# Folding products placed inside a mixture's routing head, weight rows from counting ends, and gathers queued in order of use, in a four-layer graph network

## The chip, the cores and the metric

The kernel runs on one core of one Trainium2 chip. The metric is the device time of a whole execution in microseconds (us). Five engines work side by side, each through its own queue in order: TensorE (PE, matrix products; its weight loads are listed as PEld), VectorE (DVE), ScalarE (ACT), GpSimd (POOL) and SyncE (SP). DMA transfers are issued from the queues of SP, ACT and POOL. A profile shows, for PE, the clock that was granted as a share of full speed.

## The reference, cut to what matters

512 nodes with 768 features pass four layers. Each layer adds a graph part, a mixing (attention) part and a feed-forward part to `x`. The feed-forward parts of layers 0 and 2 are mixtures of 8 experts, with 384 hidden features, in which each node goes to its one best expert:

```python
xn = _layernorm(x)
# layers 0 and 2: one expert per node (layer 0 has a router bias and gelu, layer 2 silu)
logits = xn @ Ws + bs
probs  = softmax(logits);  e = argmax(probs);  p = max(probs)
x = x + p * (act(xn @ W1[e] + b1[e]) @ W2[e] + b2[e])
# layer 1, graph part: relational attention, twice (heads = 4, then 1)
xr = einsum('nd,rdf->rnf', x, W);  qi = xr[etype, dst] @ q;  kj = xr[etype, src] @ k
# layer 3, graph part
ft = einsum('nhd,ed->nhe', h, W_fc);  a1 = (ft * attn_l).sum(-1);  a2 = (ft * attn_r).sum(-1)
```

Layer 3 ends with a mixture of 16 experts in which each expert takes 64 nodes, plus a shared expert. All arithmetic is float32 unless an intermediate is exact in a narrower type.

The scores `xr @ q` and `xr @ k` of layer 1 equal `x @ (W q)` and `x @ (W k)`. The products `W q`, `W k` depend on weights alone. The kernel computes them once per convolution and calls this folding. Layer 3's `W_fc` with `attn_l`, `attn_r` is folded in the same way.

## The kernel before

One program runs the four layers one after the other; `x` stays in on-chip memory. PE's instruction stream is in order, and a scheduler fixes the order on every engine when the program is built, from the program's order and its dependencies. `tc.issue_after(ins)` ties what is traced inside it behind `ins` on the same engine.

**Weights.** `wp` (in `Net.__init__`) is a ring of six slots of 1152 KB, tag `w`. `self.w` loads the next slot through SP's queue (L257); a load waits until the products that read that slot's former content are done. The mixtures take slots from the same ring for gathered weights. `self.gate` and `self.before` make the fifth SP load after a mixture's gathers wait for the last of these.

**PSUM.** `self.ps()` hands out eight banks in turn.

**A mixture, `moe(f, act, xn, bs)`** is called as f0 (layer 0) and f2 (layer 2). Its head:

- it normalizes `x` into `xn` (L401-405), writes `xn` to DRAM as `f_there` (L755), loads the router weights `wg` (L750), transposes `xn` into `xnT` (`to_fm`, transposes at L354), and forms the logits `lo` (L341, L333, L767);
- DVE marks each node's best expert in `g`, `gb` (L769-779). Two small products with `lower` and `onesb` (L333) count the nodes before each node, and all nodes, per expert. Out of the counts come `bl`, the blocks of 128 nodes that an expert needs, `end`, the running sum of them, and `beg`; and `place`, the position of each node in the list sorted by expert (L787-802);
- `spot` (L820) marks that position in a 0/1 matrix of 128 x 1408 for each of the four tiles of nodes. 44 products with `number` turn it round into `who`, the node numbers of each block (L825, L827);
- `own` and `low` (L832-839) find out which expert owns each of the 11 possible blocks, and so `rows`, the weight rows to fetch;
- `gT`, `wayT`, `diag` (L853-871) carry the probabilities, and later put results back in their places.

Nine blocks are always run, two more under a branch (L942). `fetch(i)` issues three gathers on POOL: the nodes `xb` (L887), then the expert's first and second weights (L881, by `rows`), and transposes `xb` to `xbT`. `first` is the first product, `middle` the activation with its transposes, `second` the second product, whose result goes to DRAM as `f_back` (L924). Round `i` of the loop runs `middle(i)`, `first(i+1)`, `fetch(i+2)`, a bias product, `second(i)`. After the loop four gathers `yb` bring the results back in node order (L949). 16 products with `wayT` and 8 with `diag` (L957, L960) finish them, and DVE and ACT add them to `x` and normalize for the next layer, tile by tile (L967-996).

**After f0** `fold` (L1195 and on) gives `products`: six loads of `g1_t1` through SP, and 36 products of 32 columns by 384 at L1204, accumulated into two banks and copied by ACT to `vt` (L1208). Then `to_fm` transposes the new `xn` into `xnT`; `turn` transposes `vt` into `V1` (L1216); and `mix1` starts with the products of `xnT` and `m1_wqkv`. `gnn1` folds its second convolution with the same function.

**After f2** `last_two` calls `fold3` first: two small loads, `wf` and `lr`, through POOL's queue (L1587, L1589), one product of them, and twelve copies of 64 x 2 by DVE into `V` (L1598). Then it transposes `xn` into `xnT`, and `gnn3` multiplies it with `V` (L341).

Of the kernel before, what the change touches and what calls it, by code (L numbers as in the profile page):

```python
# [10 lines left out]
F32 = mybir.dt.float32  # L11
BF16 = mybir.dt.bfloat16
I16 = mybir.dt.int16
I32 = mybir.dt.int32
AF = mybir.ActivationFunctionType
OP = mybir.AluOpType
# [153 lines left out]
class Net:  # L170
# [173 lines left out]
    def narrow_tm(self, four, n):  # L344

        p = self.ps()
        for t in range(NT):
            self.acc(p[:, t * n : (t + 1) * n], [(four[:, t * P : (t + 1) * P], self.fours[:, :n])])
        return p[:, : NT * n].rearrange("p (t n) -> p t n", t=NT)
# [390 lines left out]
    def moe(self, f, act, xn, bs=None):  # L740
# [5 lines left out]
        with ExitStack() as c:  # L746
# [4 lines left out]
            xnT = one.tile([P, KC, N], F32, name="xnT")  # L751
# [15 lines left out]
            nc.vector.tensor_copy(lo, self.narrow_tm(loT, E))  # L767
# [14 lines left out]
            self.acc(p[:, :32], [(self.lower, gf)])  # L782
            self.acc(p[:, 32:64], [(self.onesb, gf)])
# [10 lines left out]
            nc.vector.tensor_tensor_scan(end, self.ones[:, :E], bl, 0.0, OP.mult, OP.add)  # L794
            beg = one.tile([P, E], F32, name="beg")
# [26 lines left out]
            for i in range(NB):  # L822
                self.acc(p[:, 2 * i : 2 * i + 2], [(spot[:, t, i * P : (i + 1) * P], self.number[:, t, :]) for t in range(NT)])
# [3 lines left out]
            nc.vector.tensor_copy(who, sums)  # L827

            own = one.tile([P, NB, E], F32, name="own")
            low = one.tile([P, NB, E], F32, name="low")  # L830
            iob = self.io16[:, :NB, None].to_broadcast([P, NB, E])
            nc.vector.tensor_tensor(own, iob, end[:, None, :].to_broadcast([P, NB, E]), OP.is_lt)  # L832
            nc.vector.tensor_tensor(low, iob, beg[:, None, :].to_broadcast([P, NB, E]), OP.is_ge)
            nc.vector.tensor_mul(own, own, low)
            nc.vector.tensor_mul(low, own, self.io8[:, None, :].to_broadcast([P, NB, E]))
            which = one.tile([P, NB, 1], F32, name="which")
            nc.vector.tensor_reduce(which, low, AX.X, OP.add)
            rows = one.tile([P, NB], I32, name="rows")
            nc.vector.tensor_scalar(rows, which[:, :, 0], float(P), self.me, OP.mult, OP.add)
# [39 lines left out]
            def pick(table, i):  # L879
                t = self.wp.tile([P, WB], F32, tag="w", name="w") if i < NA else two.tile([P, WB], F32, name="wm")  # L880
                nc.gpsimd.indirect_dma_start(out=t, out_offset=None, in_=table.rearrange("e p n -> (e p) n"),  # L881
                                             in_offset=bass.IndirectOffsetOnAxis(ap=rows[:, i : i + 1], axis=0))
                return t

            def fetch(i):
                xb = two.tile([P, D], F32, name="xb", bufs=3)
                nc.gpsimd.indirect_dma_start(out=xb, out_offset=None, in_=there,  # L887
                                             in_offset=bass.IndirectOffsetOnAxis(ap=who[:, i : i + 1], axis=0))
                w1 = pick(d[f + "_w1"], i).rearrange("p (k n) -> p k n", k=KC)
                w2 = pick(d[f + "_w2"], i).rearrange("p (k n) -> p k n", k=3)  # L890
                xbT = two.tile([P, KC, P], F32, name="xbT")
                for k in range(0, KC, 3):
                    p = self.ps()
                    for j in range(3):
                        self.tr(p[:, j * P : (j + 1) * P], xb[:, (k + j) * P : (k + j + 1) * P])
                    self.copy(xbT[:, k : k + 3, :], p[:, :HW].rearrange("p (k n) -> p k n", k=3))
                return xbT, w1, w2

            def first(i, xbT, w1):
                p = self.ps()  # L900
                self.acc(p[:, :HW], [(xbT[:, k, :], w1[:, k, :]) for k in range(KC)])
                h = two.tile([P, HW], F32, name="h" if i < NA else "hm")
                self.copy(h, p[:, :HW])
                return h
# [10 lines left out]
            def second(i, hT, w2):  # L915
                y = two.tile([P, D], F32, name="y")
                for nb in range(2):
                    p = self.ps()
                    at = slice(nb * HW, (nb + 1) * HW)
                    self.acc(p[:, :HW], [(hT[:, k, :], w2[:, k, at]) for k in range(3)])  # L920
                    self.copy(y[:, at], p[:, :HW])
                if i != NA - 1:
                    o = i * P if i < NA else (i - 1) * P
                    nc.scalar.dma_start(back[o : o + P, :], y)  # L924
                return y
# [3 lines left out]
            xbT, w1, w2 = fetch(0)  # L929
            h = first(0, xbT, w1)  # L930
            ahead = fetch(1)
            for i in range(NA - 1):
                hT = middle(i, h)
                xbT, w1, after = ahead
                h = first(i + 1, xbT, w1)
                if i + 2 < NA:
                    ahead = fetch(i + 2)
# [4 lines left out]
            with tc.If(count > NA):  # L942
                for i in range(NA, NB):
                    xbT, wa, wb = fetch(i)
                    second(i, middle(i, first(i, xbT, wa)), wb)
# [245 lines left out]
    def fold(self, wq, l, H):  # L1191
# [4 lines left out]
        def products(temp):  # L1196
            vt = temp.tile([96, D], F32, name="vt")
            ps = [self.ps() for _ in range(2)]
            for kb in range(2):
                ws = [self.wr(d[f"g1_t{l}"][r, kb]) for r in range(3)]  # L1200
                for j in range(3):
                    for nb in range(2):
                        for r in range(3):
                            nc.tensor.matmul(ps[nb][32 * r : 32 * r + 32, :HW], wq[:, 3 * kb + j, :],  # L1204
                                             ws[r][:, j, nb * HW : (nb + 1) * HW],
                                             start=kb + j == 0, stop=kb == 1 and j == 2)
            for nb in range(2):
                nc.scalar.copy(vt[:, nb * HW : (nb + 1) * HW], ps[nb][:96, :HW])  # L1208
            return vt
# [9 lines left out]
        return products, turn  # L1219
# [93 lines left out]
    def gnn1(self, V1, xnT):  # L1313
        nc, tc, d = self.nc, self.tc, self.d
        with ExitStack() as c:
# [31 lines left out]
            products, turn2 = self.fold(self.padded(one.tile([P, KC, 32], F32, name="wq"), 2, 1), 2, 1)  # L1347
# [4 lines left out]
            with tc.tile_pool(name="g1_vt", bufs=1) as temp:  # L1352
                vt = products(temp)
# [161 lines left out]
    def last_two(self, xn, xnT, out):  # L1515
# [5 lines left out]
        with ExitStack() as c:  # L1521
            one = c.enter_context(tc.tile_pool(name="m3_one", bufs=1))
            two = c.enter_context(tc.tile_pool(name="m3_two", bufs=2))
            V = self.fold3(one)
# [57 lines left out]
    def fold3(self, one):  # L1582
# [9 lines left out]
        p = self.ps()  # L1592
        self.acc(p[:, : 2 * H], [(wf, lr)])
        for a in range(2):
            at = slice(64 * a, 64 * a + 64)
            for f in range(KC):
                h = 2 * f + a
                nc.vector.tensor_copy(V[at, f, h : h + H + 1 : H], p[at, h : h + H + 1 : H])  # L1598
        return V
# [332 lines left out]
def tile_net(ctx, tc, dram, at, out, only=ALL):  # L1932
# [30 lines left out]
    with tc.tile_pool(name="L1", bufs=1) as pool, ExitStack() as keep:  # L1963
        right = keep.enter_context(tc.tile_pool(name="L1n", bufs=1, side="right"))
        xn = right.tile([P, NT, D], F32, name="xn")
        net.moe("f0", AF.Gelu, xn, "f0_bs")
        right = keep.enter_context(tc.tile_pool(name="L1a", bufs=1, side="right"))
        xnT = pool.tile([P, KC, N], F32, name="xnT")
# [3 lines left out]
        products, turn = net.fold(net.wq1, 1, 4)  # L1972
        vt = products(right)
# [15 lines left out]
    with tc.tile_pool(name="f3_x", bufs=1) as last:  # L1989
# [4 lines left out]
        with tc.tile_pool(name="f3_n", bufs=1) as p2:  # L1994
            xn = p2.tile([P, NT, D], F32, name="xn")
            net.moe("f2", AF.Silu, xn)
            there = net.last_two(xn, xnT, xn)
# [26 lines left out]
```

## Time and profile before

| | us |
|---|---|
| median of 3 runs | 4235.73 |
| lowest, highest | 4232.37, 4238.52 |
| the profiled execution's own time | 4235.37 |
| its span, first to last instruction | 4233.6 |
| PE busy | 4092.9 |
| DVE busy | 1295.3 |
| ACT busy | 664.4 |
| POOL busy | 274.2 |

The span is a little shorter than the time of the same execution. A row of the timeline gives start, duration, engine, line, operation, `out<-in` with the shapes, the number of instructions that are merged in it and, in brackets, the idle time before it with what ended that. The float32 products show as two rows each: a product of 128 x 128 with 384 columns, counted x12, is six products. A row of waits gives who waited for whom: total, times, longest. A row of windows gives the busy time of PE, PEld, DVE, ACT and POOL in a stretch with their instruction counts, then the granted PE clock, the busy share of the DMA engines and GB/s.

### The profile page before, as it was taken

The numbers are of one execution on the slowest core, as the hardware profiler recorded it, in microseconds if no ns is written. First come the engines' busy times: TensorE is split into PE (matmuls) and PEld (weight loads), VectorE is DVE, ScalarE is ACT, GpSimd is POOL, SyncE is SP. The second block draws the span as 40 slices with busy tenths as digits, with TensorE's granted clock in tenths as the row PEclk, the third lists the DMA queues.
The fourth block names the chain that finished last, engine by engine and source line by source line (L and its number), as shares of the span: only waits on it lengthen the run. The fifth ranks groups of instructions, "written<-read, shape, count | busy, mean of one in ns | idle before, by whom it ended". The sixth has DMA issues, their size and how long they took to land. (4 is left out here: it accounts for less than half of the span.)

```text
span 4233.6 us, 40102 instructions
## 1 busy us (share of the span) xinstructions
PE 4092.9 (97%) x16356; PEld 2094.4 (49%) x16356; DVE 1295.3 (31%) x3096; ACT 664.4 (16%) x1258; POOL 274.2 (6%) x325
## 2 busy tenths in 40 slices
PE   9989999999989999999999999989989999999999
PEld 3434555554455566755644444445654444444444
DVE  8871111112432135613220101034751222122211
ACT  1221200001312223511200000012620000000000
POOL 1120000001022010000000000021110000000000
PEclk9999999999999999999999999989999999999999
DMA  3111011111047112211211111064069999999998
GB/s 111 53 64 56 23 45 67 68 56 54 18 178 291 42 56 72 109 45 56 98 44 57 55 56 53 4 237 155 12 282 427 427 427 426 427 427 427 420 425 366
DMA packets 99549, 710.90 MB, mean 168 GB/s; under 512 B 12608, under 2 KB 12945, under 8 KB 29985
## 3 DMA queue, kind: packets, MB, share of 16 engines
q1 hardware_dynamic: 78064, 601.20, 35.2%
q0 software_dynamic: 16816, 95.80, 6.0%
q10 hardware_dynamic: 4480, 11.28, 0.7%
q8 instruction: 132, 2.16, 0.2%
q14 instruction: 57, 0.46, 0.0%
HBM read 685.68 MB, written 22.54 MB: 167 GB/s over the span
## 5 line engine op out<-in xcount | busy, mean ns | idle before, releaser
L1851 PE MATMUL ps<-w,xg 128*64 128x384 f32 x3072 | 567.1, 489 | 0.3 <-DVE xg L249 0.3
L1851 PEld LDWEIGHTS ps<-w,xg 128*64 128x64 f32 x3072 | 235.8, 137 | 287.0 <-issue 257.5
L1473 PE MATMUL ps<-aT,w 128*128 128x512 f32 x864 | 372.3, 592 | 0.0
L1867 PE MATMUL ps<-w,hT 128*64 128x384 f32 x1536 | 319.4, 490 | 3.4 <-ACT hT L251 1.9
L333 PE MATMUL ps<-xnT,w 128*128 128x512 f32 (+1 forms) x732 | 321.5, 596 | 0.2 <-ACT xnT L251 0.2
L1473 PEld LDWEIGHTS ps<-aT,w 128*128 128x128 f32 x864 | 164.4, 190 | 203.4 <-issue 202.1
L333 PE MATMUL ps<-w,xnT 128*128 128x384 f32 x672 | 221.6, 487 | 0.2 <-DVE xnT L249 0.2
L333 PEld LDWEIGHTS ps<-xnT,w 128*128 128x128 f32 (+1 forms) x732 | 134.3, 184 | 174.7 <-issue 171.1
L1867 PEld LDWEIGHTS ps<-w,hT 128*64 128x64 f32 x1536 | 131.8, 137 | 166.7 <-issue 137.1
L410 DVE TENSOR_TENSOR x<-x,ps 128x384 f32<-128x384 f32 x224 | 123.5, 553 | 262.7 <-PE ps L333 192.7
L333 PE MATMUL ps<-C,parts 128*128 128x512 bf16 x864 | 188.6, 380 | 2.7 <-DVE inv L1495 2.7
L333 PE MATMUL ps<-w,hT 128*128 128x384 f32 x552 | 184.7, 490 | 3.9 <-ACTq L942 3.9
L514 PE MATMUL ps<-ohd,so 128*128 128x512 bf16 x816 | 184.1, 386 | 2.7 <-DVE so L511 2.7
L333 PEld LDWEIGHTS ps<-w,xnT 128*128 128x128 f32 x672 | 127.2, 190 | 88.4 <-issue 4.7
L1483 DVE TENSOR_TENSOR aT<-inv,ps 128x512 f32<-128x512 f32 x72 | 49.5, 687 | 365.6 <-PE ps L333 365.6
L1854 ACT ACTIVATE h<-ps 128x384 f32<-128x384 f32 x64 | 31.4, 490 | 781.5 <-PE ps L1851 781.5
L1855 DVE TENSOR_TENSOR h<-h,ps 128x384 f32<-128x384 f32 x64 | 35.4, 554 | 371.6 <-PE ps L1851 371.6
L333 PEld LDWEIGHTS ps<-w,hT 128*128 128x128 f32 x552 | 103.3, 190 | 81.2 <-ACT xbT L251 7.6
L333 PE MATMUL ps<-w,aT 128*128 128x384 f32 (+1 forms) x416 | 139.6, 486 | 0.5 <-DVE aT L249 0.4
L333 PE MATMUL ps<-xnT,sw 128*128 128x512 f32 x288 | 139.3, 615 | 0.0
L333 PEld LDWEIGHTS <-parts 128*128 128x128 bf16 x864 | 84.7, 98 | 108.1 <-issue 8.8
L514 PEld LDWEIGHTS <-so 128*128 128x128 bf16 x816 | 79.7, 99 | 107.6 <-DVE so L511 14.3
(511 smaller groups left out, 4826.7 us busy)
## 6 DMA issues: line engine op xcount, KB each, us to landing
w<-in_f_Wg_dram SPq DMA_DIRECT2D x128, 1152.0 KB, 14.6
w<-in_f_Wu_dram SPq DMA_DIRECT2D x128, 1152.0 KB, 14.7
w<-in_f_Wd_dram SPq DMA_DIRECT2D x128, 1152.0 KB, 14.6
w<-in_g_w_dram SPq DMA_DIRECT2D x54, 1152.0 KB, 5.1
w<-in_m_wqkv_dram SPq DMA_DIRECT2D x24, 1152.0 KB, 8.3
w<-in_g_t_dram SPq DMA_DIRECT2D x12, 1152.0 KB, 6.3
w<-in_m_wp_dram SPq DMA_DIRECT2D x8, 1152.0 KB, 5.2
ea<-in_edge_attr_dram SPq DMA_DIRECT2D x34, 256.0 KB, 2.7
```

The source lines that it names most:

```text
L333: i = self.nc.tensor.matmul(out, a, b, start=n == 0, stop=n == len(pairs) - 1)
L410: self.nc.vector.tensor_add(xs, xs, p)
L514: nc.tensor.matmul(p, so[:, n, t * P : (t + 1) * P], ohd[:, j, :], start=False, stop=j == (g + 1) * HJ - 1)
L1473: nc.tensor.matmul(outs[nb * 3 + f], w[:, k, f * P : (f + 1) * P], xT[:, k, :], start=first and k == 0, stop=last and k == KC - 1)
L1483: nc.vector.tensor_mul(aT[:, f, :], inv[:, r, :], p)
L1851: nc.tensor.matmul(p[a * 64 : a * 64 + 64, :HW], xg[:, k, a * CAP : (a + 1) * CAP], ws[b][a][:, k, :], start=k == 0, stop=k == KC - 1)
L1854: nc.scalar.activation(h, pg[:, :HW], AF.Silu)
L1855: nc.vector.tensor_mul(h, h, pu[:, :HW])
L1867: nc.tensor.matmul(po[nb][a * 64 : a * 64 + 64, :HW], hT[:, f * P + a * 64 : f * P + a * 64 + 64], wd[a][:, f, nb * HW : (nb + 1) * HW], s ...
```

## The change

Four things change, in both mixtures unless said otherwise.

1. `fold` returns `in_parts` in place of `products`: the same 36 products in three parts of 6, 12 and 18. In f0 they are handed to `moe` as `fill`, and run after the logits' products, after the two counting products, and after the `spot` products, each tied to its place with `issue_after`. Their six loads move ahead of the mixture's on SP. In `gnn1` the three parts run one after the other where `products` ran. `xnT` is made outside `moe` and passed in.
2. `fold3` splits in two. Its loads and the memset of `V` come ahead of f2's mixture on POOL's queue; the product and the twelve copies run in round 2 of f2's loop (`later`).
3. `rows` comes from `end` alone: `which` counts how many of the first seven ends a block's number has reached. `own` is made from `which` after `who`. One comparison, two multiplications and the intermediate `low` fall away. The 44 `spot` products run tile by tile instead of block by block, in one accumulation.
4. The gathers of the always-run blocks are queued with `send`, each behind the former: first weights of block 0, nodes 0, nodes 1, first weights 1, second weights 0, and then in each round nodes `i+2`, first weights `i+2`, second weights `i+1`. Transposing (`turned`) is separate from fetching.

```diff
-    def moe(self, f, act, xn, bs=None):
+    def moe(self, f, act, xn, xnT, bs=None, fill=None, later=None):
...
+            logits = self.narrow_tm(loT, E)
+            nc.vector.tensor_copy(lo, logits)
+            last = self.told
+            if fill:
+                with tc.issue_after(last):
+                    last = fill(0)
...
+            with tc.issue_after(last):
+                self.acc(p[:, :32], [(self.lower, gf)])
+                last = self.acc(p[:, 32:64], [(self.onesb, gf)]).ins
+            if fill:
+                with tc.issue_after(last):
+                    last = fill(1)
...
+            nc.vector.tensor_tensor(over, self.io16[:, :NB, None].to_broadcast([P, NB, E - 1]),
+                                    end[:, None, : E - 1].to_broadcast([P, NB, E - 1]), OP.is_ge)
+            nc.vector.tensor_reduce(which, over, AX.X, OP.add)
+            nc.vector.tensor_scalar(rows, which[:, :, 0], float(P), self.me, OP.mult, OP.add)
...
-            for i in range(NB):
-                self.acc(p[:, 2 * i : 2 * i + 2], [(spot[:, t, i * P : (i + 1) * P], self.number[:, t, :]) for t in range(NT)])
+            with tc.issue_after(last):
+                for t in range(NT):
+                    for i in range(NB):
+                        last = nc.tensor.matmul(p[:, 2 * i : 2 * i + 2], spot[:, t, i * P : (i + 1) * P],
+                                                self.number[:, t, :], start=t + i == 0,
+                                                stop=t == NT - 1 and i == NB - 1).ins
+            if fill:
+                with tc.issue_after(last):
+                    last = fill(2)
...
-            nc.vector.tensor_tensor(own, iob, end[:, None, :].to_broadcast([P, NB, E]), OP.is_lt)
-            nc.vector.tensor_tensor(low, iob, beg[:, None, :].to_broadcast([P, NB, E]), OP.is_ge)
-            nc.vector.tensor_mul(own, own, low)
-            nc.vector.tensor_mul(low, own, self.io8[:, None, :].to_broadcast([P, NB, E]))
...
+            with tc.issue_after(placed):
+                nc.vector.tensor_tensor(own, self.io8[:, None, :].to_broadcast([P, NB, E]),
+                                        which.to_broadcast([P, NB, E]), OP.is_equal)
...
+            def send(fn, *args):
+                nonlocal sent
+                with tc.issue_after(sent) if sent else nullcontext():
+                    t, i = fn(*args)
+                sent = i.ins
+                return t
...
-            xbT, w1, w2 = fetch(0)
-            h = first(0, xbT, w1)
-            ahead = fetch(1)
+            w1 = send(pick, W1, 0)
+            xb = send(gather, 0)
+            ahead = send(gather, 1)
+            h = first(0, turned(xb), w1)
+            w1 = send(pick, W1, 1)
+            w2 = send(pick, W2, 0)
+            xbT = turned(ahead)
             for i in range(NA - 1):
                 hT = middle(i, h)
-                xbT, w1, after = ahead
                 h = first(i + 1, xbT, w1)
                 if i + 2 < NA:
-                    ahead = fetch(i + 2)
+                    xb = send(gather, i + 2)
+                    w1 = send(pick, W1, i + 2)
+                after = send(pick, W2, i + 1)
+                if i + 2 < NA:
+                    xbT = turned(xb)
+                if later and i == 2:
+                    later()
                 second_bias(i // 2, i % 2)
                 second(i, hT, w2)
                 w2 = after
...
+        def in_parts(temp):
+            vt = temp.tile([96, D], F32, name="vt")
+            ps, ws = [], []
+            def part(n):
+                if n == 0:
+                    ps.extend(self.ps() for _ in range(2))
+                if n < 2:
+                    ws.append([self.wr(d[f"g1_t{l}"][r, n]) for r in range(3)])
+                kb = n // 2
+                return products(vt, ps, kb, ((0,), (1, 2), (0, 1, 2))[n], ws[kb])
+            return vt, part
...
-        net.moe("f0", AF.Gelu, xn, "f0_bs")
+        xnT = pool.tile([P, KC, N], F32, name="xnT")
+        in_parts, turn = net.fold(net.wq1, 1, 4)
+        vt, part = in_parts(right)
+        net.moe("f0", AF.Gelu, xn, xnT, "f0_bs", fill=part)
...
-        products, turn = net.fold(net.wq1, 1, 4)
-        vt = products(right)
         net.to_fm(xn, xnT)
         turn(V1, vt)
...
-            net.moe("f2", AF.Silu, xn)
-            there = net.last_two(xn, xnT, xn)
+            V, folded = net.fold3(p2)
+            net.moe("f2", AF.Silu, xn, xnT, later=folded)
+            there = net.last_two(xn, xnT, xn, V)
```

## The prediction

> **What bounds the kernel now.** I read the page first, then what TensorE (PE) waits for, then the timeline and windows of the two mixtures.
>
> ```profile
> span 4233.6 us, 40102 instructions
> PE 4092.9 (97%) x16356; PEld 2094.4 (49%) x16356; DVE 1295.3 (31%) x3096; ACT 664.4 (16%) x1258; POOL 274.2 (6%) x325
> ```
>
> PE is busy for 97% of the span, so only time that PE idles (4233.6 - 4092.9 = 140.7 us) or runs at a reduced clock can be won. Its named waits, the longest first (total, times, longest):
>
> ```profile
> PE ps L354 <- DMA xb<-f_there,who: 11.9, 2, 6.1
> PE ps L333 <- DVE spot L820: 9.6, 8, 3.7
> ...
> PE ps L333 <- DMA lr<-in_g_lr_dram: 6.7, 1, 6.7
> ...
> PE ps L1204 <- DMA w<-in_g_t_dram: 3.5, 1, 3.5
> ```
>
> All four stand around the mixtures (`moe`: f0 near 1210-1352, f2 near 2770-2915). At most some 40 us are within reach, 1%. The head of f0, from its timeline:
>
> ```profile
> 1224.86 1.17 PEld L333 LDWEIGHTS <-spot 128*128 128x128 bf16 x41 [0.47 <-DVE spot L820]
> ...
> 1226.39 0.17 DVE L827 CAST who<-sums 128x11 int32<-128x11 f32 x1
> ...
> 1226.77 1.05 POOL L881 DMA_INDIRECT w<-in_f_w_dram,rows  x1 [9.00 <-DVE g L853]
> ...
> 1228.12 0.97 POOL L887 DMA_INDIRECT xb<-f_there,who  x1 [0.30 <-issue]
> ...
> 1235.74 1.54 PE L354 MATMUL ps<-ident,xb 128*128 128x128 f32 x6 [6.08 <-DMA xb<-f_there,who]
> ...
> 1237.29 6.00 PE L333 MATMUL ps<-w,xbT 128*128 128x384 f32 x12
> ```
>
> The row gather `xb` is issued behind a weight gather, lands 7.5 us later, and PE then works at half clock. The same 12 matmuls take 4.04 us later in the loop, and six transposes 0.82 instead of 1.54. The tail of f0, where products and then transposes of `xn` follow the mixture:
>
> ```profile
> 1336.25 5.25 PE L1204 MATMUL ps<-w,wq 128*32 128x384 f32 x40
> 1341.59 1.03 ACT L979 ACTIVATE xn<-x,mv,rs 128x768 f32<-128x768 f32 x1 [0.42 <-DVE mv L970]
> 1345.03 4.06 PE L1204 MATMUL ps<-w,wq 128*32 128x384 f32 x32 [3.53 <-DMA w<-in_g_t_dram]
> 1349.02 2.84 PE L354 MATMUL ps<-ident,xn 128*128 128x128 f32 x24
> ...
> 1352.19 23.09 PE L333 MATMUL ps<-w,xnT 128*128 128x384 f32 x71
> ```
>
> And the tail of f2:
>
> ```profile
> 2908.97 0.59 PE L333 MATMUL ps<-lr,wf 64*128 64x24 f32 x2 [6.72 <-DMA lr<-in_g_lr_dram]
> ...
> 2909.66 0.15 DVE L1598 COPY V<-ps 64x2 f32<-64x2 f32 x1 [4.25 <-PE ps L333]
> ...
> 2911.99 1.03 ACT L979 ACTIVATE xn<-x,mv,rs 128x768 f32<-128x768 f32 x1 [0.62 <-DVE mv L970]
> ```
>
> The DVE copy of `V` stands in order in the middle of the norm of the last tile; it waits 4.25 us and the norm with it.
>
> **Tail of f0.** The 36 products (72 rows, 5.25 + 4.06 = 9.31 us) and the 3.53 us wait go: 12.8 us leave PE. Not all is won, since the norm becomes the limit: the last `xn` ends at 1341.59 + 1.03 = 1342.6. In the built program the two ACT copies of `V` (0.38 each) now stand between those activations and wait for the transposes of `vt`, so I add 0.65: 1343.3. From the last `xn` to the first reader of `xnT` f2's tail takes 1.6 us (2911.99 + 1.03 = 2913.0 to 2914.65). So the `xnT` products start at 1344.9 instead of 1352.2: 7.3 us. The queries' weights (`m1_wqkv`) take the place of the six `g1_t` loads on SP, whose slots come free from 1302 on; not late. [...] The windows of before (the column after POOL is the granted clock) show both outcomes:
>
> ```profile
> 1229.70:1235.70 6.00, 0.00 (x0) 0.00 (x0) 0.69 (x1) 0.00 (x0) 4.48 (x6) 0.50 0.95 327
> 1341.50:1345.00 3.50, 0.00 (x0) 0.00 (x0) 0.05 (x1) 1.03 (x1) 0.00 (x0) 1.00 1.00 284
> ```
>
> A 3.5 us pause kept full clock, the 6 us one did not. After the change PE has 24 + 6 transposes spread over 7 us there, no long pause. By the row the cost is 0[...]; I take 0.3, near the row. Gain 7.0 (5 to 8).
>
> **Head of f0.** The products run in three parts at 9.31 / 72 = 0.13 us a row. Part one, 12 rows, 1.55 us, in the 1.62 us between the logits (end 1217.66) and `gb` (1219.28). Part two, 24 rows, 3.1 us, in the 3.67 us before `spot` (1219.50 to 1223.16). Part three, 36 rows, 4.65 us, after the `spot` matmuls. PE is in order: a part that overruns its gap delays the routing chain by the excess. The margins are 0.1, 0.6 and, below, about 1 us; at half clock part one would cost 1.5. Their `g1_t` loads move ahead of SP's wait for `more`; by the rotation of six slots four have theirs by 1188, the last two when the last projection leaves its slots (1207-1209), landing by 1217 at the row's 6.3 us; needed at 1225. They compete with `wg` (issued 1209.46, 2.2 us to land, needed 1213.5, so 1.8 in hand) and the 1.5 MB write of `f_there` (1212.34, 5.4 us; even 5.5 later it precedes the gather). [...] No row here shows that contest: by the 2.2 us row it costs 0[...]. I take 0.5.
>
> The row gather comes sooner. (a) `rows` is made before `spot`, so the first weight gather leaves POOL's queue ahead of `who`: 1228.12 - 1226.77 = 1.35. Its slot opens when part two ends (1222.6), before `who`. (b) The `spot` matmuls now go tile by tile: after the last `spot` 11 remain instead of 41 (1.26 us x 30/41 = 0.9). Against it: three small DVE operations ahead of `place` (0.2 of them not in latency gaps) and the 0.68 us copy of `gT`, which the program puts before `sums` (0.3). Net 0.4. (c) Landing: 7.5 us beside a 1152 KB gather issued 1.3 us ahead; the `yb` gathers, the same shape, take 4.3. The weight gather now has 3.5 us of lead, so I take 5.0, near `yb`: 2.5 (0 to 3.2). `xb` is there at 1235.7 - 4.25 = 1231.5. Part three ends near 1225.4 + 4.65 = 1230.1, with 0.6 for `way` 1230.7: covered. (d) PE never rests, so the clock stays: 0.72 + 1.96 = 2.7. Sum 4.25 + 2.7 - 0.5 = 6.4 (3.5 to 7.3).
>
> **Head of f2.** No filler here: (a) to (c) alone, 1.35 + 0.4 + 2.5 = 4.2, the half clock stays (1.5 to 5.5). Three POOL steps (`wf`, `lr`, the memset, 1.5 us) come ahead of `io` at 2705; `io` is used at 2789.
>
> **Loop.** 16 rounds, PE without a wait at 9.76 us each, so the new queue order has nothing to win. PE's order in a round is as before. The second weights are queued one place later; their slot opens after the second product of three rounds before, some 25 us ahead of use, and the slowest weight gather took 15.5. Cost 0. The product `wf` x `lr` moves in here: 0.59 us cold, 0.3 at full clock; its 12 copies of 0.15 lie on DVE, 20% busy here. Cost 0.3 (to 1).
>
> **Tail of f2.** Without fold and copies the last norm runs as in f0's tail, where from the last pair of adds (1338.43) to the end of `xn` it took 4.2 us: 2904.37 + 4.2 = 2908.6 instead of 2913.0, so 4.4 off; 0.4 off that for the clock, which was low here too. Gain 4.0 (2 to 4.5).
>
> **The sum.** 7.0 + 6.4 + 4.2 - 0.3 + 4.0 = 21.3. All later work hangs on PE and moves up. Span 4233.6 - 21.3 = 4212.3; the profiled run took 4235.4, so 4214.1. The median of the runs, 4235.7, lies 0.4 above it: 4214.4. Edits in the second folding of layer 1 change no queue's order: 0.
>
> **Rivals.** *Second: the gathers land as late as before and the clock drops.* For it: `xb` took 6.0 to 15.2 us in all, and load stays high[...]. Against: its two slow cases each stood behind a fresh weight gather. Then the heads give 1.75 each, f0's without the clock's 2.7; tails 5 + 3: 1.75 + 1.75 + 8 - 0.3 = 11.2, hence 4224. *Third: the change doesn't do what it says*, because the products overrun their gaps: part one at half clock (+1.5), part two and three behind late loads. Then their 9.3 us are merely moved; the chain pays what the tail wins, and f2 leaves 4 to 8: about 4230. Against: 8 us between landing and use. *Fourth, slower: the second weights arrive late in each round,* since POOL queues them behind the next first weights and PE stops at `second`. Price: the lateness times 16 rounds; it decides from 21.3 / 16 = 1.33 us a round on, and at 2 us a round ends at 4247. For it: DMA is 92% busy in the loop. Against: they would have to take over 26 us where 15.5 is the longest.
>
> **How the numbers follow.** Forecast (4208 to 4220) 0.62, second 0.22, third 0.10, fourth 0.06. A measurement can tell some 0.2%, 8.5 us, from no change. Forecast, second for the most part, and a little of the third are faster: 0.87; most of the third the same: 0.08; the fourth slower: 0.05. The upper bounds of the parts sum to 7.3 + 8 + 5.5 + 4.5 = 25 and runs scatter by 3, so the range starts at 4207; it ends at 4225 so as to take in the second case and leave out the third and fourth.
>
> **What would show it.** The folding products (`w`, `wq`) among the head's rows, no wait above 1 us before `spot`, granted clock 1.00 from 1217 to 1243; `xb` issued within 0.5 us of `who` and its wait under 1.5 us in f0; the `xnT` products 7 us after the diagonal ones rather than 16; no `lr` wait. Wrong: products at 0.26 us a row, waits at `hT`'s products in the loop, `xb` landing in over 7 us.

## The result, and the profile after

| | us |
|---|---|
| before, median of 7 runs beside those of after | 4236.28 (4232.37 to 4238.52) |
| after, median of 7 runs | 4221.8 (4217.49 to 4224.51) |
| ratio, with its 95% interval | 0.9966 (0.9957 to 0.9975) |
| profiled execution of after: own time, span | 4221.8, 4219.7 |

The change makes the kernel 14.5 us faster; 21.3 were forecast, and the time lies inside the range. In a second series the same kernel took 4217.5 against 4234.7 (0.9957, 0.9943 to 0.9971), 17.2 us. So the gain is some 14 to 17 us: about three quarters of the forecast. The question is where the rest went.

The engines' busy times, first on the page of after:

```profile
span 4219.7 us, 40101 instructions
PE 4095.4 (97%) x16356; PEld 2090.6 (50%) x16356; DVE 1294.7 (31%) x3092; ACT 664.3 (16%) x1258; POOL 274.1 (6%) x325
```

PE's idle time fell from 140.7 to 4219.7 - 4095.4 = 124.3 us, by 16.4; but PE's busy time rose by 2.5 us with the same 16356 instructions. By stretch, f0 has 1.0 us more, f2 1.4 less, and 3.0 more lie in the layers between the mixtures (1.7) and behind f2 (1.3), so this sum shows no lower clock around the mixtures; the mean granted clock of the execution is 0.990, before 0.989. DVE has four instructions fewer: two multiplications fall away in each mixture, while there are two comparisons as before. Waits of PE in after that stand around the mixtures:

```profile
PE ps L354 <- ACT xn L1018: 6.3, 6, 1.4
...
PE ps L842 <- DVE spot L837: 4.8, 2, 3.8
...
PE ps L341 <- DMA wg<-in_f_wg_dram: 3.6, 1, 3.6
...
PE ps L354 <- DMA xb<-f_there,who: 3.0, 1, 3.0
...
PE ps L333 <- DMA bd<-in_g_res_dram: 0.7, 1, 0.7
...
PE ps L999 <- DMA yb<-f_back,slot: 0.5, 1, 0.5
```

The waits for `lr` (6.7 us) and for `g_t` (3.5) are gone, that for `xb` fell from 11.9 to 3.0, that for `spot` from 9.6 to 4.8. Four are new: the router's product waits 3.6 us for `wg`, the f2 tail waits for `bd`, the transposes of `xn` wait for the norm, and the diagonal products wait 0.5 us for `yb`. The router's product in the head of f0, from the timeline of before:

```profile
1209.46 0.35 ACTq L750 DMA_DIRECT2D wg<-in_f_wg_dram  x1
...
1213.47 2.25 PE L341 MATMUL ps<-xnT,wg 128*32 128x512 f32 x12 [0.24 <-DVE xnT L249]
```

The head of f0, from the timeline of after:

```profile
1206.99 2.91 SPq L257 DMA_DIRECT2D w<-in_g_t_dram  x2
...
1209.62 0.36 ACTq L751 DMA_DIRECT2D wg<-in_f_wg_dram  x1
...
1217.02 3.51 PE L341 MATMUL ps<-xnT,wg 128*32 128x512 f32 x12 [3.63 <-DMA wg<-in_f_wg_dram]
...
1222.39 1.49 PE L1239 MATMUL ps<-w,wq 128*32 128x384 f32 x12
...
1224.23 2.78 PE L1239 MATMUL ps<-w,wq 128*32 128x384 f32 x24
...
1230.24 5.76 PE L1239 MATMUL ps<-w,wq 128*32 128x384 f32 x36
...
1231.17 1.39 POOL L904 DMA_INDIRECT xb<-f_there,who  x1 [2.25 <-DVE own L855]
...
1236.21 0.50 PE L354 MATMUL ps<-ident,xb 128*128 128x128 f32 x3
...
1237.72 4.14 PE L333 MATMUL ps<-w,xbT 128*128 128x384 f32 x12 [0.22 <-issue]
```

The three parts of the fill (x12, x24, x36) stand where they should, and the first two fit their gaps. But `wg` is issued at 1209.62 and used at 1217.02, 7.4 us later; before it was 1213.47 - 1209.46 = 4.0, and its landing took 2.2. Two loads of `g_t` are issued by SP at 1207.0 and 1209.6, just ahead of it. All later steps are late by that, and the clock suffers. Windows over the same stretch, one of before, then four of after (the last three columns are granted clock, busy share of the DMA engines, GB/s):

```profile
1209.00:1213.00 4.00, 3.15 (x27) 2.66 (x24) 2.59 (x7) 0.46 (x2) 3.30 (x4) 1.00 0.10 29
```

```profile
1209.00:1213.00 4.00, 3.15 (x25) 2.61 (x24) 2.43 (x7) 0.30 (x2) 3.14 (x4) 1.00 1.01 415
1213.00:1217.00 4.00, 0.40 (x4) 0.17 (x3) 1.77 (x3) 2.84 (x4) 3.79 (x4) 0.98 0.99 393
1217.00:1220.50 3.50, 3.48 (x12) 0.64 (x12) 0.00 (x0) 0.00 (x0) 0.91 (x2) 0.53 0.47 184
...
1230.00:1236.00 6.00, 6.00 (x48) 2.13 (x47) 2.61 (x11) 0.47 (x1) 3.92 (x4) 0.72 0.88 289
```

From 1209 to 1217 the DMA engines are full; in the kernel before they moved 29 GB/s in the first 4 us of this. After the pause of 3.63 us the clock is at 0.53, so that the router's product takes 3.51 instead of 2.25 us. The other three places did what the prediction said. The diagonal products in the tail of f0 (8 rows, so four products), in before:

```profile
1333.57 2.74 PE L960 MATMUL ps<-yb,diag 128*128 128x384 f32 x8
```

The tail of f0 in after:

```profile
1333.67 2.85 PE L999 MATMUL ps<-yb,diag 128*128 128x384 f32 x8 [0.49 <-DMA yb<-f_back,slot]
1336.36 1.32 PE L354 MATMUL ps<-ident,xn 128*128 128x128 f32 x6
1338.67 0.87 PE L354 MATMUL ps<-ident,xn 128*128 128x128 f32 x6 [1.00 <-ACT xn L1018]
...
1342.89 1.33 PE L354 MATMUL ps<-ident,xn 128*128 128x128 f32 x6 [0.93 <-ACT xn L1018]
1344.01 8.24 PE L333 MATMUL ps<-w,xnT 128*128 128x384 f32 x21
```

The `xnT` products start 1344.01 - 1336.52 = 7.5 us after the diagonal ones end (before: 1352.19 - 1336.31 = 15.9). Yet the first 21 take 8.24 us, where 71 took 23.09 before (0.325 each, so 6.8): 1.4 us go to a lower clock (granted 0.74 from 1344 to 1349). The gather and its use in the head of f2, in before:

```profile
2794.62 0.98 POOL L887 DMA_INDIRECT xb<-f_there,who  x1 [0.30 <-issue]
...
2801.99 1.54 PE L354 MATMUL ps<-ident,xb 128*128 128x128 f32 x6 [5.81 <-DMA xb<-f_there,who]
```

The head of f2 in after:

```profile
2781.87 1.04 POOL L898 DMA_INDIRECT w<-in_f_w_dram,rows  x1 [80.84 <-DVE at L817]
...
2785.27 0.15 DVE L851 CAST who<-sums 128x11 int32<-128x11 f32 x1
...
2786.28 1.00 POOL L904 DMA_INDIRECT xb<-f_there,who  x1 [3.37 <-DVE b L858]
...
2790.47 1.54 PE L354 MATMUL ps<-ident,xb 128*128 128x128 f32 x6 [3.00 <-DMA xb<-f_there,who]
2792.00 5.03 PE L333 MATMUL ps<-w,xbT 128*128 128x384 f32 x12
```

The weight gather is away before `who`, and `xb` is there 4.2 us after its issue instead of 7.4. In the tail of f2 the fold is gone, but a load on POOL now ends last:

```profile
2896.28 1.54 PE L354 MATMUL ps<-ident,xn 128*128 128x128 f32 x6 [1.02 <-ACT xn L1018]
2897.75 2.17 PE L341 MATMUL ps<-xnT,V 128*32 128x512 f32 x8
2898.09 0.52 POOL L1672 DMA_DIRECT2D bd<-in_g_res_dram  x1 [2.44 <-DMA mask<-M]
...
2900.58 0.67 PE L333 MATMUL ps<-bd,xnT 128*128 128x256 f32 x2 [0.67 <-DMA bd<-in_g_res_dram]
```

The gain by stretch, each between two marks that both kernels have, from the timelines (us; the last two columns are the changed kernel in the second series and the second run of one experiment, below):

| stretch | forecast | after | after, second series | `wg` early |
|---|---|---|---|---|
| f0, first transposes to the second `first` | 6.4 | -0.3 | 2.1 | 6.7 |
| f0, from there to the first copy of `v` in layer 1 | 7.0 | 7.3 | 7.6 | 7.0 |
| f2, `gb` to the first `m3` products | 7.9 | 8.5 | 8.1 | 6.7 |

In after these make 15.5. The remainder (0.2 lost ahead of f0, 0.2 won between the mixtures, 1.7 lost behind f2) brings it to 13.9, the difference of the spans. The 1.7 is this execution's: from the first `m3` products to the end of the span after took 1305.4 us, before 1303.8, and the second series' execution of the changed kernel 1304.0. The f2 stretch scatters most: its code is the same in three further executions below, which gain 7.1, 6.7 and 5.4 there.

### The profile page after: what moved, and what is told of

Same layout as the page of the kernel before. It is cut to its first block, busy times and chain, and to the rows that moved or that the text cites. A ratio compares the mean times of both kernels' runs of the same rounds, so it can differ in the third digit from the quotient of the medians.

```text
span 4219.7 us, 40101 instructions
## 1 busy us (share of the span) xinstructions
PE 4095.4 (97%) x16356; PEld 2090.6 (50%) x16356; DVE 1294.7 (31%) x3092; ACT 664.3 (16%) x1258; POOL 274.1 (6%) x325
## 6 DMA issues: line engine op xcount, KB each, us to landing
w<-in_f_Wd_dram SPq DMA_DIRECT2D x128, 1152.0 KB, 14.5
```

## The experiments

Theory W: the head of f0 gained nothing because `wg` landed late behind the last two `g_t` loads. Against it stood P (the fill's parts overrun their gaps, and in-order PE holds the chain), O (the order of the gathers gains nothing in f0), and, for what was left over, C (the clock that drops in short pauses). There were three series, each with its own runs of the kernel before: medians 4234.7, 4233.8 and 4236.1.

### The changed kernel again

> The changed kernel once more, beside the experiments of this series. Both theories: 4221.8 again (within 2 us); the router's product in the head of f0 waits some 3.6 us for wg, and the first products over expert rows start near 1237.7.

Measured: 4217.5 (4214.7 to 4219.6), ratio 0.9957 (0.9943 to 0.9971). The wait for `wg` is there again, 3.7 us. First products over expert rows at 1236.89. What differs from the first execution is the first block: there part three ran partly at a lower clock (5.76 us, granted 0.72 from 1230 to 1236) and PE had no wait for `xb` behind it, where here it waits 1.61 us; and two pauses of 0.93 and 0.80 us before the `h` transposes and the second `first`, marked "issue" in the first execution, are absent here. That is 2.4 us of scatter in the head with the same program; the cause of the two pauses stays open.

### `wg` early

```diff
         make_identity(nc, self.ident)
+        self.wg0 = keep.tile([P, KC, 32], F32, name="wg")
+        nc.scalar.dma_start(self.wg0.rearrange("p k e -> p (k e)"), dram["f0_wg"])
...
-            wg = one.tile([P, KC, 32], F32, name="wg")
-            nc.scalar.dma_start(wg.rearrange("p k e -> p (k e)"), d[f + "_wg"])
+            wg = self.wg0 if f == "f0" else one.tile([P, KC, 32], F32, name="wg")
+            if f != "f0": nc.scalar.dma_start(wg.rearrange("p k e -> p (k e)"), d[f + "_wg"])
```

> The changed kernel, but the router's weights wg of f0 are loaded at the very start into a tile of their own, so nothing on the ACT queue stands in the contest with the g1_t loads. Theory W (wg landed late because the last two g1_t loads were in front of it; the 4.8 us that the logits came late, and the half clock after that pause, ate the gain of f0's head): the router's product waits for nothing, the logits are back at about 1216.6, the first products over expert rows start at 1231.5 to 1232.5 instead of 1237.7, and the time is 4215 to 4217.5. Rival P (the fill's parts overrun their gaps and hold the chain, whatever wg does): the logits come sooner but the first products start no more than 1.5 us sooner; 4220.5 to 4222.

> The kernel of e1_early_wg once more, beside the two refined fillers. Theory W: ratio to before 0.9946 again (4209 to 4213); the router's product waits for nothing.

Measured: 4212.2 (4209.5 to 4217.6), ratio 0.9946 (0.9932 to 0.996), beside 4217.5 of the changed kernel in the same series; and again, in the third series, 4212.6 (4210.7 to 4213.6), ratio 0.9943 (0.993 to 0.9957). The intervals still overlap with that of the changed kernel, so the size is read from the traces. The head of f0 in that last run, from its timeline:

```profile
1211.81 2.25 PE L341 MATMUL ps<-xnT,wg 128*32 128x512 f32 x12 [0.24 <-DVE xnT L249]
...
1223.77 4.07 PE L1239 MATMUL ps<-w,wq 128*32 128x384 f32 x36
...
1229.58 0.52 PE L354 MATMUL ps<-ident,xb 128*128 128x128 f32 x3 [1.36 <-DMA xb<-f_there,who]
...
1230.74 4.14 PE L333 MATMUL ps<-w,xbT 128*128 128x384 f32 x12
```

The head starts at 1207.72 in this execution. The router's product follows after 4.09 us, as in the kernel before, and the first products over expert rows after 23.0 instead of 28.2 (changed kernel) or 27.9 (before). The fill's parts take 1.49, 2.78 and 4.07 us, PE waits 1.36 us for `xb` behind them, and the granted clock is 1.00 from 1211 to 1236. The head gains 6.7 us over before, and 6.5 in the first run of this kernel. P falls: the same parts in the same places cost the chain nothing once `wg` is on time. The one load of 96 KB is worth about 5 us: 28.2 - 23.0 = 5.2 in the traces, 5.3 by the medians of the first series.

### The fill back in the tail

```diff
-        net.moe("f0", AF.Gelu, xn, xnT, "f0_bs", fill=part)
+        net.moe("f0", AF.Gelu, xn, xnT, "f0_bs")
+        for n in range(3):
+            part(n)
```

> The changed kernel, but the 36 folding products of layer 1 stand after the mixture f0 again, with their loads; rows by counting, the order of the transfers, the split of f2's fold stay. Both theories: wg is on time, since the g1_t loads are not in the head. If the head of f0 gains from the order of the transfers what the head of f2 gained (5.7), it starts its first products near 1231.6, the tail gives back 7.1, and the time is 4221.8 - 6.2 + 7.1 = 4222.7 (4221.5 to 4224). If the head of f0 gains nothing from the order of the transfers (rival O), 4228 to 4229.5.

Measured: 4221.7 (4219.7 to 4227.4), ratio 0.9971 (0.996 to 0.9981). From its timeline:

```profile
1208.78 2.13 PE L354 MATMUL ps<-ident,xn 128*128 128x128 f32 x18
...
1231.90 6.39 PE L333 MATMUL ps<-w,xbT 128*128 128x384 f32 x12
```

O falls: without the fill, `wg` on time, the first products start at 1231.90, 23.1 us after the head's first transposes, as with the fill and `wg` early. They then take 6.39 us instead of 4.14, and the six transposes ahead of them 1.54 instead of the 0.82 of the next six; up to the second `first` the head gains 4.4 over before. The tail has the products and their 3.46 us wait for `g_t` again. Within this series, by the medians, the fill is worth 4221.7 - 4217.5 = 4.2 us as the change has it, and 4221.7 - 4212.2 = 9.5 with `wg` early.

### The loads alone

Six loads of `g1_t`, read by nothing, ahead of f0 in the kernel before:

```diff
+        for kb in range(2):
+            for r in range(3):
+                net.wr(net.d["g1_t1"][r, kb])
         net.moe("f0", AF.Gelu, xn, "f0_bs")
```

> The kernel before, with six loads of g1_t (the ones that the fill would use) queued on SP ahead of the mixture f0 and read by nothing; the products and their own loads stay in the tail. Theory W: the two loads that get their slots last stand in front of wg, the router's product waits 3 to 4 us for it, and the time is 3.5 to 5 us above before: 4239.5 to 4241.5. Rival P: loads without products cost nothing, 4236 (within 1).

Measured: 4234.9 (4232.9 to 4240.4), ratio 1.0002 (0.9994 to 1.001). It tells nothing about W: unread loads found their slots much sooner. The last two went out on SP some 88 us before `wg`, from the timeline of this run:

```profile
1118.82 0.81 SPq L257 DMA_DIRECT2D w<-in_g_t_dram  x2
```

So the next run held two such loads back by a dependency on the last two tiles of the last projection (`marks` are the last products of these tiles; `gate` ties a load to one):

```diff
-                    self.acc(p[:, :HW], [(aT[:, h, t * P : (t + 1) * P], ws[h // 4][:, h % 4, :]) for h in range(8)]
+                    ins = self.acc(p[:, :HW], [(aT[:, h, t * P : (t + 1) * P], ws[h // 4][:, h % 4, :]) for h in range(8)]
...
-                    self.add_x(t, nb, p[:, :HW])
+                    self.add_x(t, nb, p[:, :HW]); self.marks = [old, ins.ins] if nb + t else [ins.ins] * 2; old = ins.ins
...
+        for r in range(2): net.gate, net.before = net.marks[r], 0; net.wr(net.d["g1_t1"][r, 1])
         net.moe("f0", AF.Gelu, xn, "f0_bs")
```

> The kernel before, with two loads of g1_t that nothing reads, each held until the last two tiles of the last projection ahead of f0 are done, so that SP issues them where the changed kernel issues its last two (about 2.5 us ahead of wg and with it). Theory W (those loads in front of wg make it late): wg takes 5 to 8 us from issue to use instead of 2.2, the router's product waits 3 to 4 us, and the time is 3 to 5 us above that of the kernel before. Rival (the loads are not the reason): wg is on time and the time within 1 us of before.

Measured: 4237.9 (4234.6 to 4241.3), 4.0 above the 4233.8 of before, ratio 1.0009 (1.0001 to 1.0017). From its timeline:

```profile
1206.79 0.38 ACTq L750 DMA_DIRECT2D wg<-in_f_wg_dram  x1
1206.91 0.35 SPq L257 DMA_DIRECT2D w<-in_g_t_dram  x1
...
1214.79 3.63 PE L341 MATMUL ps<-xnT,wg 128*32 128x512 f32 x12 [4.23 <-DMA wg<-in_f_wg_dram]
```

W holds, with nothing else of the change in the kernel. The first of the two loads was issued at 1201.58, 5.2 us ahead of `wg`; from 1202.3 to 1206.3 the DMA engines moved 295 GB/s, 1.18 MB, as much as the whole load, so it was all but done. A single 1152 KB load issued 0.12 us behind `wg` was enough to make it take 8.0 us from issue to use. Its landing took 7.9 us, and 7.3 in the second series' execution of the changed kernel, against 2.2 in the kernel before. One share is not separated: the 1536 KB write of `f_there`, issued 2.9 us behind `wg` on the same queue, is in flight by then too. It takes 8.0 us to land in after instead of 5.4, and in this run some 8.8 (an estimate: 7.1 is the median of the two mixtures' writes, and f2's took 5.4 in the kernel before). Without the loads `wg` is down, after 2.2 us, before that write is issued, so the loads are needed for the delay; how long it would be without the write is open.

### The fold back in f2's tail

```diff
-            V, folded = net.fold3(p2)
-            net.moe("f2", AF.Silu, xn, xnT, later=folded)
+            net.moe("f2", AF.Silu, xn, xnT)
...
+            V, folded = self.fold3(one)
+            folded()
             self.to_fm(xn, xnT)
```

> The changed kernel, with the fold of wf and lr back in f2's tail (loads, product and 12 copies), everything else kept. The prediction priced the split at 4.0 less 0.3 in the loop: 3.7 us slower than the changed kernel. Theory C (the clock that drops in the norm without the fold takes a part back): 2 to 3 us slower. Rival (the fold lay under the norm anyway): within 0.7.

Measured: 4225.0 (4218.3 to 4228.8), ratio 0.9976 (0.9965 to 0.9986); the changed kernel had 0.9966 and 0.9957 in the other series, so 4 to 8 us slower by the medians, with runs that scatter by 10. In the profile, that of the fastest of its eight runs, the wait for `lr` is back:

```profile
2892.35 0.59 PE L333 MATMUL ps<-lr,wf 64*128 64x24 f32 x2 [7.24 <-DMA lr<-in_g_lr_dram]
```

From the products of `gb` to the first `m3` products f2 takes 139.4 us, instead of 135.5 and 135.9 in the changed kernel. But the same f2 code took 136.9 us with the fill back in the tail, and 137.4 and 138.6 with `wg` early. Against these five executions the split is worth 0.7 to 3.8 us, 2.5 in the mean; 3.7 were forecast, 2 to 3 by C. That it gains is shown; the size is not told apart.

### Holding the clock

Products of an `xn` tile and the identity, read by nothing, were put into PE's pauses of the kernel with `wg` early; first in the tails of f0 and f2, and in another kernel in f2's head by way of `fill`:

```diff
+            if warm and t < NT - 1:
+                with self.tc.issue_after(end): last = [self.nc.tensor.matmul(ps[KC][:, :HW], self.ident, x[:, t, :HW], start=True, stop=True).ins for _ in range(warm)][-1]
...
+            def warm(n):
+                p = net.ps()
+                for _ in range((4, 9, 12)[n]):
+                    i = nc.tensor.matmul(p[:, :HW], net.ident, xn[:, 0, :HW], start=True, stop=True)
+                return i.ins
+            net.moe("f2", AF.Silu, xn, xnT, fill=warm, later=folded)
```

> The kernel of e1_early_wg, with three products of an xn tile and the identity, read by nothing, after the transposes of each of the first three tiles in the tails of f0 and f2. Theory C (in the changed kernel the transposes are spread so thinly over the norm that the clock drops, 1.3 us in f0's tail and 1.1 to 3.8 in f2's): granted clock 1.00 in both tails, f2's stretch from the narrow product of V to the first m3 products 15.2 us instead of 19.0 (e1) and 16.5 (changed kernel), time 2 to 5 us below e1. Rival N (the stretch waits for bd's loads or the norm whatever the clock does, or the added products hold the transposes): within 1 us of e1, or above it.

> The kernel of e1_early_wg, with 4, 9 and 12 products of an xn tile and the identity, read by nothing, at the three places of f2's head where f0 has its folding products. Theory C: the clock stays at 1.00, the xb transposes take 0.82 instead of 1.54 and the first products over expert rows 4.1 instead of 5.0 to 5.6 us, and the time is 1.5 to 2.5 us below e1. Rival P (filler in the gaps holds the routing chain): the start of the xb transposes comes 1 us or more later after gb than in e1, and the time is that of e1 or above.

Measured: 4222.7 (ratio 0.9968) and 4218.3 (0.996), against 0.9946 and 0.9943 for the kernel they were built on: both medians are slower, by 6 to 11 us, though the intervals still touch. By the products' times the clock was held in f2's head (the first products 4.04 us instead of 5.02) and in f0's tail (the first copy of `v` 4.1 us after the first `xnT` product instead of 5.7), but not all through f2's tail: three filler products took 3.89 us there, and the next three 2.10. The filler was twice as long as meant (a float32 product of 384 columns shows as two rows of 0.35 us), and in the tails it also needed a seventh PSUM bank that the adds still held (a wait of 1.53 us for DVE). In f2's head the last filler took 7.99 us, and `xb`'s transposes came 15.5 us after `gb` instead of 11.8. This is P's price, seen where it is real: PE's order passes on what filler overruns, 3.7 us here. Smaller ones followed, without the extra bank:

```diff
-                for _ in range((4, 9, 12)[n]):
+                for _ in range((2, 4, 4)[n]):
...
+                with self.tc.issue_after(end): last = [self.nc.tensor.matmul(ps[0][:, (t + 1) * P :], self.ident, x[:, t, : (NT - 1 - t) * P], start=True, stop=True).ins for _ in range(warm[t])][-1]
```

> As e4_warm_tails, with its two faults mended: the added products (1 of 384 columns, 2 of 256, 3 of 128 after the first three tiles) fit the pauses of 1.0 to 1.45 us at two passes of 0.35 us for 384 columns, and they write columns of the transposes' own PSUM tile that are overwritten later, so they wait for no buffer. Theory C: the xn transposes start as in e1, the granted clock stays at 1.00, f2's stretch from the narrow product of V to the first m3 products takes 15.2 to 16 us, and the time is 1.5 to 4 us below e1. Rival N: within 1 us of e1.

> As e5_warm_head with 2, 4 and 4 products instead of 4, 9 and 12 (0.7 us each), which fit the gaps. Theory C: from gb to the xb transposes 11.8 us as in e1, these take 0.82 instead of 1.54, the first products over expert rows 4.1 instead of 5.0 to 5.6, and the time is 1.5 to 2.5 us below e1. Rival P: the xb transposes come 1 us or more later after gb, time as e1 or above.

Measured: 4213.6 (ratio 0.9947) and 4213.8 (0.9948), against 4212.6 of the kernel they were built on in the same series: no difference that can be told. With the fillers in the tails the products' times show no drop of the clock in either: the last six transposes of `xn` in f2's tail took 0.88 us instead of 1.54, the product with `V` 1.56 instead of 2.30, and in f0's tail the first copy of `v` came 4.2 us after the first `xnT` product instead of 5.7. In f2's head the third filler took 4.52 us where the second, of the same length, took 2.83; behind it three of the six `xb` transposes took 0.52, where six had taken 1.54, and the first products 4.14 instead of 5.02. But in f2's tail what was won went into the next wait, for `bd`:

```profile
2890.79 1.56 PE L341 MATMUL ps<-xnT,V 128*32 128x512 f32 x8 [0.33 <-DVE xnT L249]
2893.94 0.67 PE L333 MATMUL ps<-bd,xnT 128*128 128x256 f32 x2 [1.59 <-DMA bd<-in_g_res_dram]
```

So time is lost there to the clock, as C has it (granted 0.57 in after, from 1344 to 1347 and from 2896 to 2900), at some 0.7 to 1.5 us a place; that the whole kernel gains by holding it is not shown.

### All together

`wg` early, both small fillers, and `bd`'s four loads on POOL ahead of those of `mask` and `C`:

```diff
-        nc.gpsimd.dma_start(mask, self.M16[3])
-        for t in range(NT):
-            nc.gpsimd.dma_start(C[:, t, 0, :], self.T16[t])
         bd = one.tile([P, 2, P], F32, name="bd")
         nc.gpsimd.memset(bd, 0.0)
...
                 nc.gpsimd.dma_start(bd[b * 64 : b * 64 + 64, n, b * 64 : b * 64 + 64], d[a])
+        nc.gpsimd.dma_start(mask, self.M16[3])
+        for t in range(NT):
+            nc.gpsimd.dma_start(C[:, t, 0, :], self.T16[t])
```

> The changed kernel with wg early, both fillers of e4b and e5b, and bd's four loads queued on POOL ahead of the mask's and C's. If theories W and C hold and add up: 3 to 6 us below e1, no wait for bd, f0 and f2 at full clock throughout; ratio to before 0.993 to 0.994. If the clock comes back by itself in most executions: within 1.5 us of e1.

Measured: median 4210.2 (4208.1 to 4221.2), ratio 0.9946 (0.9933 to 0.996). The wait for `bd` is gone:

```profile
2887.28 1.56 PE L341 MATMUL ps<-xnT,V 128*32 128x512 f32 x8 [0.33 <-DVE xnT L249]
2888.92 0.67 PE L333 MATMUL ps<-bd,xnT 128*128 128x256 f32 x2
```

From `gb` to the first `m3` products f2 takes 133.9 us instead of 137.4 with `wg` early alone, and the span, 4206.8 us, is the shortest of all. That the clock would be full throughout was expected too and did not come: in f2's head three of the `xb` transposes took 0.86 us instead of 0.52, and the first products 4.89 instead of 4.14. The medians differ by 2.4 us, and the intervals overlap, that of the changed kernel (0.9943 to 0.9971) included; that this version beats the kernel before is certain, not that it beats `wg` early alone.

## Why the prediction was right or wrong

**Right: the direction, the mechanism, and four of five terms.** In the profile of after the waits fell where it said. Tail of f0: 7.0 forecast, 7.3 and 7.6 measured (the loop included). Head of f2: 4.2 forecast; the wait for `xb` alone gave 16.2 - 11.7 = 4.5 from the products of `gb` to its transposes, and the clock came back a little sooner (first products 5.03 us instead of 6.25). Split of the fold: 3.7 forecast with its cost in the loop, 0.7 to 3.8 by the fold put back. The loop: the second weights were never late, the rounds stayed at 9.76 us; the fourth rival did not occur (its 4247 adds up to 4246).

**Wrong: the term for `wg` in the head of f0.** The prediction named the contest, put it at 0 by the row, and took 0.5, an estimate of its author that no row showed, counting 1.8 us in hand. Measured, the router's product came 3.4 us late in after: seven times the 0.5. With the 1.8 in hand that is 5.2 us more of landing; the second series' execution shows it directly, 7.3 us instead of 2.2. The lower clock that followed (0.53) took 1.3 more on that product alone. The measured delay is about what a whole 1152 KB load takes (5.3 us), with the write of `f_there` in it, which the prediction had weighed only for the gather behind it. With it goes the step "PE never rests, so the clock stays": the pause for `wg` was itself the rest. The run with `wg` early gives the term its size without this mistake: 6.7 measured, where the forecast was 6.4 with its 0.5 for the contest and 6.9 without. The late `wg` does not make up all of the miss in after. Its head is 7.05 us longer than with `wg` early: 4.6 are the later logits, 0.5 part three at a lower clock (0.72), and 1.9 mostly the two pauses whose cause is open. In the second series the head is 4.65 longer, and the logits alone are 4.4 late.

**Luck in the range.** 4221.8 lies outside the 4208 to 4220 given to the forecast itself, and nearer to the second rival's 4224 than to 4214.4; the range took it in because its upper end had been set for that rival. The rival's cause is not what the traces show: the gathers did land sooner, in 4.2 us in f2, and the low clock in f0 came with the late `wg`. The second series' 4217.5 lies inside the forecast's own stretch.

**Right by offset: the clock in the tail of f0.** Taken at 0.3, near the row that showed full clock after a pause of 3.5 us; about 1.4 in after. No long pause stood there: PE's pauses between the transposes were 0.93 to 1.00 us, and the granted clock still went from 1.00 (1336.5 to 1340) to 0.74 (1344 to 1349). The loss went unnoticed in the sum since the start of the `xnT` products came sooner than forecast: the last `xn` was done 6.3 us behind the diagonal products, not 7.0, and the first product followed 1.2 us later instead of 1.6. That won 1.1, and the clock lost 1.1 more than its 0.3.

**The signs named ahead.** No wait above 1 us before `spot`: wrong (3.63 for `wg`). Clock 1.00 from 1217 to 1243: wrong (0.53, 0.72). `xb` issued within 0.5 us of `who`: right in f0 (0.27); its wait under 1.5 us: right in after, 1.61 in the second series. `xnT` products 7 us after the diagonal ones: 7.5. No wait for `lr`: right.

**Not foreseen:** "all later work hangs on PE and moves up" left out POOL. Since PE comes sooner to f2's tail, the last of `bd`'s loads, queued behind `mask` and `C`, ends last: 0.67 us in after, 1.59 with the small fillers in the tails.

## What to carry to other kernels

Before a bulk prefetch is moved ahead of a stage, list the small loads that the stage starts with and that are issued on any queue in the 5 us around it: they need to be gone before the bulk load goes out, even where they go by another queue. Here a load of 96 KB took 7.9 us to land instead of 2.2 with a load of 1152 KB issued 0.12 us behind it, while one issued 5.2 us ahead was all but done. Work moved into a gap is free only as long as it fits; check its length against a row of the same shape, because in-order PE hands the excess on: a filler of 7.99 us put the transposes of `xb` 15.5 us behind `gb` instead of 11.8. And after a wait is removed, look which transfer on a third engine ends next (here `bd` on POOL, 0.67 to 1.59 us).

## What the runs showed of the hardware

- A load of 96 KB took 7.3 to 7.9 us to land beside a load of 1152 KB on another engine's queue (and a write of 1536 KB issued 2.9 us later), even when it was issued 0.12 us before that load; alone, in the kernel before, it took 2.2. In the changed kernel a load of 1152 KB beside it took 5.3 us, and the DMA engines were full during it (393 to 415 GB/s).
- The granted clock fell without a long pause. In the tail of f2 three pauses of 1.0, 1.45 and 1.0 us with six transposes between them brought it down: it was 1.00 in the first three groups of transposes and 0.51 in the last, which took 1.54 us instead of 0.87, and the next product of eight rows took 2.17 instead of 1.56 us. Products of 0.8 to 1.0 us in these pauses kept it at 1.56. A single pause in front of full work went either way: 3.53 us in f0's tail of the kernel before kept full clock (1.00 from 1345 to 1349); after 3.63, 3.86 and 4.23 us of waiting for `wg` (after, the fold back in f2's tail, the two held loads) the router's product took 3.51, 3.33 and 3.63 us instead of 2.25, with 0.53 granted in after.
- The same program's head of f0 differed by 2.4 us between two executions, in part by two pauses, 0.93 and 0.80 us, that no wait explains.
